# Sums over states three half steps late instead of two, a fifth state buffer, and softplus's product split into two stages

## The chip, the cores and the metric

The kernel runs on one core of a Trainium2 chip. Times are device microseconds of that core. Five things matter on it: the tensor engine (PE), which multiplies and transposes into the accumulation memory (PSUM, eight banks per partition); the vector engine (DVE); the scalar engine (ACT); GpSimd (POOL); and the queue of the sync engine (SP), which issues the transfers. Each engine works off its own instructions in the order in which the program holds them, and waits on semaphores of the others.

## The reference, cut to what matters

An image of 128 channels and 32 by 32 pixels goes through four layers, 32 images in all: a 3x3 convolution, a Mamba block that scans the 1024 pixels in four directions, an attention layer with two short Mamba blocks, and a small circuit. Layer 1 takes nearly all the time. For each direction it does this, with 256 inner channels `d` and 16 states `n`:

```python
uc = silu(conv(in_proj(x)))                      # 256 x 1024
dtr, Bt, Ct = split(x_proj @ uc)                 # 8, 16 and 16 rows
dt = softplus(dt_proj_w @ dtr + dt_proj_b)       # 256 x 1024
def step(h, t):                                  # over the 1024 pixels
    h = exp(dt[t] * A) * h + (dt[t] * uc[t]) * Bt[t]
    y[t] = sum over n of h[:, n] * Ct[t, n]
```

After that come `y + uc * D`, a gate with `silu(z)`, the output projection, and the sum over directions.

## The kernel before, in words

Channels lie on the 128 partitions and the 1024 pixels along the free axis, so the 256 inner channels make two halves `h`. A **half step** is one state `n` of one half of one direction: 16 x 2 = 32 half steps a direction, 128 an image, 4096 for layer 1, and 64 more for the attention layer. `Steps.run` walks through all of them in one long list. Half step `i` consists of

- `decay` (L633, ACT): `da = exp(dt * A)`, in one of five buffers;
- `spread` (L653 or L647, PE): the row `Bt[n]`, copied over the partitions into a pair of PSUM banks `bu`, of which there are two pairs. In 11 half steps of 32 (`TURNED`) ACT has already multiplied by `du` in transposed form (`scale`, L662), and PE only transposes;
- `input` (L669, DVE): `bu = du * bu`, in the 21 half steps that are not turned;
- `scan` (L677, DVE): the recurrence along 1024 pixels, from `da` and `bu` into a buffer `hh`;
- `weigh` (L686, POOL): `hh = hh * cc`, where `cc` is the row `Ct[n]`, loaded by SP (L625) into one of three buffers;
- `add` (L722, PE): eight transposes add `hh` to the sums `y` in two PSUM banks. For `n = 0`, `add` first starts `y` with the product of `uc` and `D` (L701), and the sum of that state follows an iteration later (`catch_up`). When `n = 15` is in, ACT copies `y` out (`evict`, L740).

The order within iteration `i` is written out: `evict`, `decay(i+3)`, the pending reads of PSUM, `spread(i+1)`, `catch_up`, `scan(i)`, pending reads, `input(i+1)`, then **a slot for other work**, `scale(i+4)`, `weigh(i)`, `add(i-2)`, `load(i+3)`. So in PE's queue the sum of state `i-2` stands right ahead of the spread of state `i+2`.

The slot is filled by `Plan.slot`. All work outside the scans is cut into `Stage`s, in streams with a start, an end and gaps: the projections of the next direction (L280, two stages of two products for each of four blocks), `small` (L299), `rates` (softplus: L377 and the lines to L411), `turns` (L434), the gates (L481), `finish` (L459), the convolution of the next image (L969, six stages of three products), the output projection (L1021). The planner goes by estimated costs per engine (`load_of` gives those of the half step itself) and by how near each stream's end is. It looks at no measured time: the result is a fixed order.

Stages that need PSUM take one of two `mm` banks with `k.mm()`. The reading of a bank by ACT or DVE is put off with `k.later` and emitted by `k.flush`, or at once when a third bank is asked for. In `rates` the first stage, `rate`, takes both banks in one slot: one product for each 512 pixels, each of which ACT then reads twice (L385 and L386).

Buffers are by tag: `BUFS` gives four to `hh`, two to `dbl` (the projected rows: `dtr`, `Bt`, `Ct`, which the two `rates` of a direction read), each of 4 KB a partition. In the attention layer a tile `t1` shares the tag `dbl`.

Of the kernel before, what the change touches and what calls it, by code (L numbers as in the profile page):

```python
# [23 lines left out]
DS = 16  # L24
# [142 lines left out]
class Work:  # L167


    BUFS = {  # L170
        "uc": 4, "dt": 3, "du": 3, "dut": 2, "parts": 2, "dbl": 2, "cc": 3, "da": 5, "hh": 4,
        "bt": 2, "but": 3,
    }

# [67 lines left out]
class Direction:  # L242
# [116 lines left out]
    def rates(self, h, at=0):  # L359

        k, m, T = self.k, self.m, self.T
        nc = k.nc
        t = {}

        def new(tag):
            return k.work.tile([P, T], F32, tag=tag, name=tag)

        def rate():  # L370
            self.dt[h], self.du[h] = new("dt"), new("du")
            t["relu"], t["w"] = new("relu"), new("w")
            k.rating = True
            for c, cs in enumerate(self.chunks):
                at = 32 * (2 * h + c)
                ps = k.mm(self.ch)
                nc.tensor.matmul(  # L377
                    ps, m.dw[at : at + 32, h * P : (h + 1) * P], self.dbl[at : at + 32, cs],
                    start=True, stop=True,
                )  # L380
                k.later(parted(cs, ps))

        def parted(cs, ps):
            def run():
                nc.scalar.activation(self.du[h][:, cs], ps, AF.Abs)  # L385
                nc.scalar.activation(t["relu"][:, cs], ps, AF.Relu)  # L386
            return run

        def expo():
            k.exps()  # L390
            nc.scalar.activation(self.du[h], self.du[h], AF.Exp, scale=-1.0)

        def rounded():
            nc.scalar.activation(t["w"], self.du[h], AF.Identity, bias=k.one)
            nc.scalar.activation(t["w"], t["w"], AF.Identity, bias=k.less)  # L395

        def log():
            k.exps()
            nc.scalar.activation(self.dt[h], self.du[h], AF.Ln, bias=k.one)

        def lost():
            nc.gpsimd.tensor_tensor(t["w"], t["w"], self.du[h], ALU.subtract)  # L402

        def whole(name, op, last=False):
            def run():
                nc.gpsimd.tensor_tensor(self.dt[h], self.dt[h], t[name], op)  # L406
                k.rating = not last
            return run

        def weighed():  # L410
            nc.gpsimd.tensor_tensor(self.du[h], self.dt[h], self.uc[h], ALU.mult)  # L411

        return [
            Stage(rate, pe=1.2, act=2.4, takes=True, at=at, when=lambda: not k.rating),
            Stage(expo, act=1.2, gap=2),
            Stage(rounded, act=2.3), Stage(log, act=1.2), Stage(lost, pool=2.4),
            Stage(whole("relu", ALU.add), pool=2.4), Stage(whole("w", ALU.subtract, True), pool=2.4),
            Stage(weighed, pool=2.4),
        ]
# [135 lines left out]
class Steps:  # L555
# [11 lines left out]
    def run(self, ways, plan):  # L567

        k = self.k
        steps = [(w, h, n) for w in ways for h in range(2) for n in range(DS)]  # L570
        self.steps = steps
        for i in range(3):
            self.load(i)
        for i in range(3):
            self.decay(i)
        self.spread(0)
        self.input(0)
        for i in range(len(steps) + 2):
# [12 lines left out]
            self.add(i - 2)  # L591
            self.load(i + 3)
        self.evict()
        k.flush()
# [4 lines left out]

    def load_of(self, i):  # L600

        n = (i - 2) % DS
        pe, act, pool, dve = 1.05, 1.15, 2.4, 2.3
        if n < 2:

            pe += 1.05
        if n == 0:
            act += 1.2
        if self.has(i + 1):
            pe += 1.0 if self.turned(i + 1) else 0.5  # L610
# [132 lines left out]
class Kernel:  # L743
# [173 lines left out]
    def images(self):  # L917
        tc, nc, d = self.tc, self.nc, self.d
        with ExitStack() as ctx:
# [162 lines left out]
            images, ways, plan = [], [], Plan(self)  # L1082
# [20 lines left out]
            with tc.manual_schedule():  # L1103
                w = ways[0]
# [10 lines left out]
                each = Steps.SLOTS  # L1115
                for k, w in enumerate(ways):
                    j, q = divmod(k, 4)
                    at = k * each
                    if w.last:
                        plan.add(w.gates(), at - 11, at + 14)  # L1120
                        plan.add(w.finish(0), at + 19, at + 31)
                    if q == 2:
                        plan.add(ways[k - 1].finish(1) + way_out(images[j], ways[k - 1]), at + 3, at + 16)
                    if q == 0 and j:
                        plan.add(ways[k - 1].finish(1) + way_out(images[j - 1], ways[k - 1]), at + 3, at + 16)
# [13 lines left out]
    def attention(self):  # L1139
# [4 lines left out]
        with ExitStack() as ctx:  # L1144
# [14 lines left out]
            chunks = [(c, slice(c * ch, (c + 1) * ch)) for c in range(T // ch)]  # L1159
            biases = [self.vec("L2_conv_convh_b"), self.vec("L2_conv_convw_b")]  # L1160
            g8s, ways = [], []
            both8 = self.work.tile([8, 2, T], F32, tag="carry", name="g8")
            for a, m in enumerate(ms):
# [6 lines left out]
                for c, cs in chunks:  # L1170
# [5 lines left out]
                        self, m, 0, taps, lambda c, taps=taps: taps(3, c), view, T, segment=S  # L1176
# [59 lines left out]
            with tc.manual_schedule():  # L1236
                each = Steps.SLOTS
# [7 lines left out]
                for a, w in enumerate(ways):  # L1245
                    plan.add(w.gates(), a * (each + 8) + 1, a * each + 14)
                    plan.add(maps(a), a * each + 4, a * each + 28)
                    plan.add(w.finish(0), a * each + 19, a * each + 31)
# [3 lines left out]
                plan.add(ways[0].finish(1) + way_out[: len(chunks)], each + 3, each + 9)  # L1252
                plan.add(way_out[len(chunks) :], each + 10, 2 * each - 2)
# [294 lines left out]
```

## Time and profile before

| | us |
|---|---|
| median of 3 runs | 15073.83 (15066.03 to 15084.82) |
| the profiled execution, its own time | 15093.06 |
| its span, first to last instruction | 15091.3 |
| busy: PE / DVE / ACT / POOL | 13174.8 / 13401.1 / 12256.2 / 12747.8 |
| mean granted clock of PE | 0.92 |

Busy times are over the whole span. The forty slices of the page are even from the second on (DVE 9 or 8 tenths, PE 8) until the last three, where the circuit runs. In groups of the page, "busy, mean ns" is the time of the group and of one instruction; what follows the bar is the idle time of the engine just ahead of these instructions and who ended it. A product of f32 appears as two rows of PE. Matmuls are pipelined, so the mean of one row is longer than the distance from row to row. The starts of one image's scans follow those of the last by 443.8 us in most images.

### The profile page before, as it was taken

The numbers are of one execution on the slowest core, as the hardware profiler recorded it, in microseconds if no ns is written. First come the engines' busy times: TensorE is split into PE (matmuls) and PEld (weight loads), VectorE is DVE, ScalarE is ACT, GpSimd is POOL, SyncE is SP. The second block draws the span as 40 slices with busy tenths as digits, with TensorE's granted clock in tenths as the row PEclk, the third lists the DMA queues.
The fourth block names the chain that finished last, engine by engine and source line by source line (L and its number), as shares of the span: only waits on it lengthen the run. The fifth ranks groups of instructions, "written<-read, shape, count | busy, mean of one in ns | idle before, by whom it ended". The sixth has DMA issues, their size and how long they took to land. (4 is left out here: it accounts for less than half of the span.)

```text
span 15091.3 us, 197699 instructions
## 1 busy us (share of the span) xinstructions
PE 13174.8 (87%) x70318; PEld 8507.7 (56%) x70318; DVE 13401.1 (89%) x8776; ACT 12256.2 (81%) x21181; POOL 12747.8 (84%) x6529
## 2 busy tenths in 40 slices
PE   7888888888888888988888888888888888888876
PEld 4555555555555555555555555555555555555532
DVE  7999989999989999898999999999999999999774
ACT  6888888888888888888888888888888888888642
POOL 6888888888888888888888888888888888888764
PEclk8999999999999999999999999999999999999877
DMA  3444444444444444444444444444444444444431
GB/s 118 159 155 155 156 153 154 156 159 156 155 153 153 158 155 159 154 154 154 153 157 159 154 157 153 155 152 158 157 157 154 155 153 154 157 159 157 144 107 68
DMA packets 633895, 2277.61 MB, mean 151 GB/s; under 512 B 77481, under 2 KB 81145, under 8 KB 632777
## 3 DMA queue, kind: packets, MB, share of 16 engines
q1 hardware_dynamic: 630600, 2263.06, 43.8%
q8 instruction: 554, 9.08, 0.2%
q14 instruction: 437, 3.57, 0.1%
q10 hardware_dynamic: 2304, 1.90, 0.0%
HBM read 2221.35 MB, written 43.33 MB: 150 GB/s over the span
## 5 line engine op out<-in xcount | busy, mean ns | idle before, releaser
L686 POOL TENSOR_TENSOR hh<-hh,cc 128x1024 f32<-128x1024 f32 x4160 | 9771.8, 2366 | 1752.5 <-DVE hh L677 1086.5
L677 DVE TENSOR_TENSOR_SCAN hh<-da,bu 128x1024 f32<-128x1024 f32 x4160 | 9415.4, 2280 | 618.6 <-PE bu L647 234.9
L722 PEld LDWEIGHTS y<-cbig,hh 128*128 128x128 f32 x33280 | 4065.2, 150 | 1793.5 <-issue 1285.2
L722 PE MATMUL y<-cbig,hh 128*128 128x128 f32 x33280 | 4762.6, 290 | 181.8 <-POOL hh L686 181.4
L633 ACT ACTIVATE da<-dt,m_na 128x1024 f32<-128x1024 f32 x4096 | 4607.2, 1144 | 352.8 <-DVE hh L677 344.9
L669 DVE TENSOR_TENSOR bu<-du,bu 128x1024 f32<-128x1024 f32 x2752 | 3336.8, 1213 | 680.5 <-PE bu L653 679.6
L662 ACT ACTIVATE but<-dut,bt 128x128 f32<-128x128 f32 x11264 | 3433.6, 392 | 0.0
L653 PE MATMUL bu<-parts,sel 48*128 48x512 bf16 x5504 | 1761.5, 402 | 638.6 <-DVE hh L677 630.0
L280 PE MATMUL mm<-hpad,m_wc 128*128 128x512 f32 x4096 | 2063.6, 627 | 104.1 <-ACT relu L386 68.6
L647 PE MATMUL bu<-cbig,but 128*128 128x128 f32 x11264 | 1606.7, 290 | 378.1 <-DVE hh L677 331.6
L647 PEld LDWEIGHTS bu<-cbig,but 128*128 128x128 f32 x11264 | 1388.4, 151 | 445.2 <-issue 287.8
L280 PEld LDWEIGHTS mm<-hpad,m_wc 128*128 128x128 f32 x4096 | 710.1, 193 | 908.6 <-issue 753.5
L653 PEld LDWEIGHTS <-sel 48*128 48x128 bf16 x5504 | 322.6, 95 | 1149.9 <-DVE hh L677 687.2
L402 POOL TENSOR_TENSOR w<-w,du 128x1024 f32<-128x1024 f32 x260 | 613.8, 2361 | 38.3 <-ACT w L395 38.3
L299 PE MATMUL mm<-uc,m_xw 128*128 128x512 f32 x1024 | 602.9, 720 | 31.0 <-ACT sz L762 22.6
L701 PEld LDWEIGHTS y<-m_skip,uc 128*128 128x128 f32 x4096 | 554.4, 212 | 132.8 <-issue 79.8
L762 ACT ACT_TABLE_LOAD x483 | 619.7, 1283 | 8.5
L768 ACT ACT_TABLE_LOAD x483 | 619.7, 1283 | 8.5
L439 ACT COPY dut<-mm 128x512 f32<-128x512 f32 x512 | 294.9, 576 | 407.0 <-PE mm L434 406.9
L406 POOL TENSOR_TENSOR dt<-dt,w 128x1024 f32<-128x1024 f32 x260 | 615.3, 2366 | 0.2
L411 POOL TENSOR_TENSOR du<-dt,uc 128x1024 f32<-128x1024 f32 x260 | 614.3, 2363 | 0.2
L406 POOL TENSOR_TENSOR dt<-dt,relu 128x1024 f32<-128x1024 f32 x260 | 613.9, 2361 | 0.0
(219 smaller groups left out, 10394.3 us busy)
## 6 DMA issues: line engine op xcount, KB each, us to landing
cc<-rows SPq DMA_DIRECT2D x4160, 512.0 KB, 3.8
xt<-in_x SPq DMA_DIRECT2D x32, 512.0 KB, 5.9
x<-xt SPq DMA_DIRECT2D x32, 512.0 KB, 3.7
xt<-x SPq DMA_DIRECT2D x32, 512.0 KB, 4.0
out<-xt SPq DMA_DIRECT2D x32, 512.0 KB, 2.9
rows<-dbl SPq DMA_DIRECT2D x130, 64.0 KB, 4.3
stats<-st SPq DMA_DIRECT2D x32, 36.0 KB, 1.5
means<-stats SPq DMA_DIRECT2D x1, 1152.0 KB
```

The costliest lines, as they stand in the source:

```text
L280: nc.tensor.matmul(self.view(ps), m.wc[:, v, j, h * P : (h + 1) * P], self.taps(j, c), start=(j == 0), stop=(j == 3),)
L406: nc.gpsimd.tensor_tensor(self.dt[h], self.dt[h], t[name], op)
L633: k.nc.scalar.activation(t, w.dt[h], AF.Exp, scale=w.m.na[:, h, n : n + 1])
L647: k.nc.tensor.matmul(t[:, b * P : (b + 1) * P], but[:, b], k.ident, start=True, stop=True, is_transpose=True,)
L653: k.nc.tensor.matmul(t[:, cs], k.sel[:, n], w.parts[:, cs], start=True, stop=True)
L662: k.nc.scalar.activation(t[:, b], w.dut[h][:, b], AF.Copy, scale=w.bt[:, b, n : n + 1])
L669: k.nc.vector.tensor_tensor(t, w.du[h], t, ALU.mult)
L677: k.nc.vector.tensor_tensor_scan(way(t), way(self.da.pop(i)), way(self.bu.pop(i)), 0.0, ALU.mult, ALU.add)
L686: k.nc.gpsimd.tensor_tensor(t, t, self.cc.pop(i), ALU.mult)
L722: k.nc.tensor.matmul(self.y[g][: w.bl, b], t[:, at], k.ident, start=False, stop=(n == DS - 1 and b == w.per - 1), is_transpose=True,)
L762: self.nc.scalar.activation(*args, AF.Silu, **kw)
L768: self.nc.scalar.preload_act_table_set("natural_log_exp_and_others")
```

## The change

Three things are changed.

1. `add(i - 2)` becomes `add(i - 3)`; the loop of `run` goes one iteration further, and `load_of` takes its `n` from `i - 3`. `hh` gets a fifth buffer, so that a state may be kept one half step longer. `dbl` gives its second buffer for it.
2. `rate` is now two stages, one for each 512 pixels, with one bank each; the planner is told 0.9 of PE and 1.2 of ACT for each (it was 1.2 and 2.4 for both).
3. The streams that read finished sums (`finish`, `way_out`, `end`) start one slot later, and most of their ends move by one.

```diff
-        "uc": 4, "dt": 3, "du": 3, "dut": 2, "parts": 2, "dbl": 2, "cc": 3, "da": 5, "hh": 4,
+        "uc": 4, "dt": 3, "du": 3, "dut": 2, "parts": 2, "dbl": 1, "cc": 3, "da": 5, "hh": 5,
...
-        def rate():
-            self.dt[h], self.du[h] = new("dt"), new("du")
-            t["relu"], t["w"] = new("relu"), new("w")
-            k.rating = True
-            for c, cs in enumerate(self.chunks):
+        def rate(c, cs):
+            def run():
+                if c == 0:
+                    self.dt[h], self.du[h] = new("dt"), new("du")
+                    t["relu"], t["w"] = new("relu"), new("w")
+                    k.rating = True
                 at = 32 * (2 * h + c)
                 ps = k.mm(self.ch)
...
-            Stage(rate, pe=1.2, act=2.4, takes=True, at=at, when=lambda: not k.rating),
+            *(
+                Stage(rate(c, cs), pe=0.9, act=1.2, takes=True, at=at, when=lambda c=c: c or not k.rating)
+                for c, cs in enumerate(self.chunks)
+            ),
...
-        for i in range(len(steps) + 2):
+        for i in range(len(steps) + 3):
...
-            self.add(i - 2)
+            self.add(i - 3)
...
-        n = (i - 2) % DS
+        n = (i - 3) % DS
...
-                        plan.add(w.finish(0), at + 19, at + 31)
+                        plan.add(w.finish(0), at + 20, at + 31)
...
-                        plan.add(ways[k - 1].finish(1) + way_out(images[j], ways[k - 1]), at + 3, at + 16)
+                        plan.add(ways[k - 1].finish(1) + way_out(images[j], ways[k - 1]), at + 4, at + 17)
...
-                        plan.add(end(images[j - 1]), at + 17, at + 44)
+                        plan.add(end(images[j - 1]), at + 18, at + 45)
```

The remaining lines of the diff make the same shift by one for the other `way_out` of layer 1 and for `finish` and `way_out` of the attention layer.

More of the change, by code (lines that the diff above doesn't have):

```diff
@@ L381, in rate @@
                 k.later(parted(cs, ps))
+            return run
         def parted(cs, ps):
@@ L1120, in images @@
                         plan.add(w.gates(), at - 11, at + 14)
-                        plan.add(w.finish(0), at + 19, at + 31)
+                        plan.add(w.finish(0), at + 20, at + 31)
                     if q == 2:
-                        plan.add(ways[k - 1].finish(1) + way_out(images[j], ways[k - 1]), at + 3, at + 16)
+                        plan.add(ways[k - 1].finish(1) + way_out(images[j], ways[k - 1]), at + 4, at + 17)
                     if q == 0 and j:
-                        plan.add(ways[k - 1].finish(1) + way_out(images[j - 1], ways[k - 1]), at + 3, at + 16)
-                        plan.add(end(images[j - 1]), at + 17, at + 44)
+                        plan.add(ways[k - 1].finish(1) + way_out(images[j - 1], ways[k - 1]), at + 4, at + 17)
+                        plan.add(end(images[j - 1]), at + 18, at + 45)
                     if q == 1 and j + 1 < self.n:
@@ L1247, in attention @@
                     plan.add(maps(a), a * each + 4, a * each + 28)
-                    plan.add(w.finish(0), a * each + 19, a * each + 31)
+                    plan.add(w.finish(0), a * each + 20, a * each + 31)
                 plan.add(ahead[begun:], 1, each - 2)
@@ L1251, in attention @@
                 way_out = out(0)
-                plan.add(ways[0].finish(1) + way_out[: len(chunks)], each + 3, each + 9)
-                plan.add(way_out[len(chunks) :], each + 10, 2 * each - 2)
+                plan.add(ways[0].finish(1) + way_out[: len(chunks)], each + 4, each + 10)
+                plan.add(way_out[len(chunks) :], each + 11, 2 * each - 2)
                 Steps(self).run(ways, plan)
```

## The prediction

> **What bounds the kernel now.** I read the page's busy times first, then its groups, then the waits of DVE and of PE, then one image in windows, then the timeline of its worst places. From the page:
>
> ```profile
> PE 13174.8 (87%) x70318; PEld 8507.7 (56%) x70318; DVE 13401.1 (89%) x8776; ACT 12256.2 (81%) x21181; POOL 12747.8 (84%) x6529
> ...
> L686 POOL TENSOR_TENSOR hh<-hh,cc 128x1024 f32<-128x1024 f32 x4160 | 9771.8, 2366 | 1752.5 <-DVE hh L677 1086.5
> L677 DVE TENSOR_TENSOR_SCAN hh<-da,bu 128x1024 f32<-128x1024 f32 x4160 | 9415.4, 2280 | 618.6 <-PE bu L647 234.9
> L669 DVE TENSOR_TENSOR bu<-du,bu 128x1024 f32<-128x1024 f32 x2752 | 3336.8, 1213 | 680.5 <-PE bu L653 679.6
> ```
>
> All engines are 81 to 89% busy; none is full. DVE sets the pace: POOL mostly waits for its scans (1086.5 us), and DVE waits for PE's spreads. The waits:
>
> ```profile
> DVE bu L669 <- PE bu L653: 679.6, 520, 53.9
> DVE hh L677 <- PE bu L647: 234.9, 185, 2.7
> ...
> PE y L722 <- POOL hh L686: 181.4, 168, 3.0
> PE mm L280 <- ACT relu L386: 68.6, 31, 2.2
> PE mm L459 <- ACT uc L762: 68.1, 31, 2.3
> ```
>
> The first two (total, times, longest, us) are what the change can win: 914.5 us, less 53.9 for the start, is 860.6 us or 27 us an image. The next three are times when PE itself stood. Only the third is on POOL; the fourth, 31 times 2.2 us, comes once an image. So PE's own load must make most of DVE's wait. One image and five stretches of it (columns: length, then busy PE, PEld, DVE, ACT, POOL):
>
> ```profile
> 4536.00:4980.00 444.00, 391.18 (x2164) 255.18 (x2162) 407.12 (x251) 377.34 (x656) 389.33 (x198) 0.95 0.47 157
> 4603.00:4616.00 13.00, 13.00 (x73) 8.24 (x72) 10.15 (x7) 8.23 (x18) 13.00 (x7) 1.00 0.35 110
> 4659.00:4669.00 10.00, 10.00 (x60) 7.27 (x61) 7.42 (x6) 5.96 (x13) 9.76 (x7) 0.96 0.34 109
> 4741.00:4779.00 38.00, 35.50 (x152) 20.33 (x151) 26.50 (x17) 28.87 (x50) 24.18 (x12) 0.96 0.39 132
> 4827.00:4845.00 18.00, 15.70 (x106) 11.08 (x104) 14.53 (x10) 16.82 (x31) 10.66 (x5) 1.00 0.46 149
> 4868.00:4881.00 13.00, 11.91 (x66) 7.44 (x65) 11.49 (x7) 11.20 (x12) 12.73 (x6) 1.00 0.57 192
> ```
>
> DVE idles 36.9 us in the image, and 2.85, 2.58, 11.50, 3.47 and 1.51 us of it in these five stretches (A to E). In A, B and C PE is full: too much other work fell into a few half steps. D and E show PE standing:
>
> ```profile
> 4830.79 1.13 PE L377 MATMUL mm<-dbl,m_dw 32*128 32x512 f32 x4
> ...
> 4835.03 0.61 ACT L386 ACTIVATE relu<-mm 128x512 f32<-128x512 f32 x1
> ...
> 4835.69 1.98 PE L280 MATMUL mm<-hpad,m_wc 128*128 128x512 f32 x4 [2.21 <-ACT relu L386]
> ...
> 4840.03 1.23 DVE L669 TENSOR_TENSOR bu<-du,bu 128x1024 f32<-128x1024 f32 x1 [1.66 <-PE bu L653]
> ...
> 4869.36 1.10 PE L722 MATMUL y<-cbig,hh 128*128 128x128 f32 x8 [1.09 <-POOL hh L686]
> ...
> 4871.03 1.23 DVE L669 TENSOR_TENSOR bu<-du,bu 128x1024 f32<-128x1024 f32 x1 [0.34 <-PE bu L653]
> ```
>
> In D softplus has both banks, the next projection waits 2.21 us for one, and DVE's product is late. In E the sum waits 1.09 us for POOL, but only 0.34 us of that reaches DVE.
>
> **What the Trainium skill says.** "Perfetto Trace Analysis", section Identifying Performance Opportunities, has the busiest of the vector, scalar and GpSimd engines as the one to follow through its gaps, and takes repeated gaps as a sign that buffers may be short: DVE at 89% with gaps that recur in each image agrees. The same page, section Matmuls, wants independent products to rotate through PSUM banks so that one is read while the next is filled: stretch D shows what it costs where they don't. "TensorE: Matmul & The Clock Gate", Part 1, has PE at half clock after an idle window of some 3.4 us; here the mean granted clock is 0.92, and in this image eight transposes of a sum take 1.91 us after PE's wait of 2.29 us on ACT in stretch C, 1.03 elsewhere. A wait of PE is thus paid twice in places.
>
> **The change part by part.** No work is removed: both built programs hold the same PE, DVE and POOL instructions. ACT gets two more switches each way between its tables, 4 x 1.283 us (rows L762 and L768), hidden in an engine 81% busy. I count per image, times 31 (32 less start and end).
>
> *Sums three behind.* Each sum asks for POOL's result one half step later. An unhindered half step lasts 3.5 us with a product (1.21 + 2.28) and about 2.2 without, against a longest wait of 3.0 us, so nearly all of PE's 181.4 us of waiting goes. What is it worth? Bounds: all 181, if each microsecond reached DVE, and 57, what I get by following DVE's late instructions back through PE's queue to such waits. I take 60. Behind the waiting sum stands the spread of state `i+2`, for which DVE waits; later are then only POOL's own tasks, which have slots of margin. The scan's wait for a free `hh` doesn't change: it needs the sum of `i-5` (was `i-4`), issued in iteration `i-2` both times. SP's loads wait on `weigh`, which isn't moved.
>
> *One buffer for `dbl`.* Its next writer is ACT after `small`, at half steps 1, 34, 68 and 99 of the new order; the last reader, the second product of `rates(1)`, stands at 127, 26, 58 and 92, two or more earlier in PE's own queue, and the transfer of the rows (4.3 us) some 25 half steps before. Cost nothing; if that cover were gone, PE's order alone would still put reader ahead of writer. `t1` comes 16 half steps after the last reader.
>
> *Two stages of softplus.* The work is the same, but no stage holds both banks. The wait of 2.2 us (68.6 in all) goes: the first product stands at 80, the second at 81, the next projection at 87. But in half step 80 the planner now puts an image product, the second output projection and the first softplus product together, some 0.9 + 1.9 + 0.9 us, and the output projection still waits for DVE (59.1 us in all, 1.9 an image). D goes from a mean of 4.9 over the images to about 3: 1.9 x 31 = 58.
>
> *The new order, C.* In half steps 58 to 66 PE has about 14.5 us of spreads and sums (9 x 1.5, plus turned ones). Before, it also has six convolution stages (2.74 each), two projection stages (1.9 each), a `finish` and two `turns` (1.8 together), softplus (1.85) and a start of `y` (1.95): 25.8, plus 2.3 of waiting. DVE needs 28.5. 42.6 less 28.5, less some 3 that PE may be ahead, is 11: the 11.5 seen. In the new order these half steps hold 20.4: 34.9 less 28.5 less 3 is 3.4. But stages five and six, the start of `y` and both `small` (1.88 each) then fall into 67 to 70, some 11 us against 2 before. I take 8 for all of C: 3.5 x 31 = 108.
>
> *The new order, A and B.* The four projection stages of A move from 18, 19, 20, 21 to 18, 19, 21, 22, and the next four from 24 to 27 to 28 to 31: PE has no run left that exceeds DVE's pace by 3. A goes from 3.0 to 0.5: 78. In B `small` and the gate no longer share a half step: 2.5 to 1, 47. On the other side, at 124 to 0 of the next image and at 93 to 96, projection, `turn` and the second softplus product now meet, 2.7 to 3.3 above DVE's pace: I add 2.3, -71.
>
> Sum: 60 + 58 + 108 + 78 + 47 - 71 = 280 us. Waits taken from one place partly come back in the next, and I see the ones that vanish better than the ones that appear; I keep three quarters, 210. From the span, 15091.3 - 210 = 14881; the profiled execution (15093.06) stood 19 above the median, so **14865 us**, 1.4% less.
>
> **Rivals.**
>
> *Only the cured waits count (20%).* The planner's order is as crowded as before, since the same PE work must fit between the same scans, and only POOL's and softplus's waits go, a part of 181 + 69: 60 to 90 us, about 15000. For it: C's work moves by a few half steps and doesn't go. Against: A and B thin out.
>
> *More than that (12%).* PE keeps its clock, and most of the 27 us an image goes: DVE's own work and bubbles need 416, so half of the rest, 13 x 31 = 400 us, gives 14670.
>
> *No difference (8%).* DVE's waits move one for one into the new crowds: 15074.
>
> *Slower (12%).* The crowd at 66 to 70 meets a PE at half clock. It now follows light half steps (56 to 58 hold 0.4 to 0.9 us of other work each), in which PE stands. About 22 us of PE work stand there; at half clock throughout, they cost up to 22 more. It decides the sign from 7 us an image on, that is if PE stays at half clock for some 14 us of those 22; at 10 us it gives 15170. For it: the clock was 0.63 from 4749 to 4753 us, in C, right after a wait. Against: over the whole of each of the five stretches it is 0.96 or 1.00 (the column after POOL).
>
> **How the numbers follow.** My forecast (14750 to 14980) has 48%. Runs here spread by 19 us, 0.13%, so 0.2% or 30 us is about what a measurement can tell from no change. Faster by that: 48 + 20 + 12 = 80%; within: 8%; slower: 12%. For 8 in 10 I leave out half of the strongest gain below and most of the slower case above: 14710 to 15075.
>
> **What would show it.** Right: PE's wait on `hh` L686 near nothing; that of L280 on L386 gone; DVE's two waits on spreads down from 914 to about 700; POOL's and DVE's busy times unchanged; an image in about 437 us; the largest gap late in C, at half steps 66 to 70. Wrong: DVE's waits on L653 as large as before with PE full around them (first rival), or PE's rows at twice the distance there (slower).

## The result: no difference

| | before | after |
|---|---|---|
| median of 12 runs, us | 15078.97 (15066.03 to 15084.82) | 15085.10 (15047.41 to 15099.89) |
| the profiled execution, its own time | 15093.06 | 15085.33 |
| its span | 15091.3 | 15083.2 |
| mean granted clock of PE | 0.92 | 0.918 |

The ratio of the times is 1.0000, with a 95% interval from 0.9991 to 1.0009. The forecast was 14865 us, a gain of 1.4%. The likeliest case (14750 to 14980) and the wider range (14710 to 15075) both miss, and the case that came true ("no difference") had a chance of 8%.

In the changed kernel the lines after softplus stand five further down: L686 is L691, L677 is L682, L722 is L727, L1021 is L1026. The page after, busy times and costliest groups:

```profile
PE 13325.4 (88%) x70318; PEld 8474.9 (56%) x70318; DVE 13424.2 (89%) x8776; ACT 12262.2 (81%) x21185; POOL 12759.8 (85%) x6529
...
L691 POOL TENSOR_TENSOR hh<-hh,cc 128x1024 f32<-128x1024 f32 x4160 | 9781.5, 2368 | 1800.8 <-DVE hh L682 1037.6
L682 DVE TENSOR_TENSOR_SCAN hh<-da,bu 128x1024 f32<-128x1024 f32 x4160 | 9416.1, 2281 | 767.4 <-PE bu L652 224.5
L674 DVE TENSOR_TENSOR bu<-du,bu 128x1024 f32<-128x1024 f32 x2752 | 3335.6, 1212 | 426.3 <-PE bu L658 422.3
```

DVE's idle time ahead of its products fell from 680.5 to 426.3 us, as it should. Ahead of its scans it rose, from 618.6 to 767.4, though the spreads' part of that did not. So something else is late. The waits of DVE (total, times, longest, us):

```profile
DVE bu L674 <- PE bu L658: 422.3, 350, 53.3
DVE hh L682 <- PE bu L652: 224.5, 125, 7.0
...
DVE hh L682 <- PE y L727: 122.6, 95, 2.8
...
DVE o L1032 <- PE mm L1026: 94.6, 33, 3.9
```

The two waits on spreads fell from 914.5 to 646.8 us, by 268, even further than the 700 that the prediction named as its sign. The third row was not among the waits before; the fourth was 3.6 us there. These two take back 214. Four smaller ones (the scan on an image product of L852, on the scaled rows of L667 and on softplus's `du`, and L986 on L974) rose by some 48 more, DVE's busy time rose by 23, and its wait on the gates' product (L465) lost 23. That closes the balance within a few us of the span's 8: DVE idles 39.3 us an image before and 39.0 after, as a mean over the images. And the waits of PE:

```profile
PE mm L974 <- ACT xpad L961: 95.1, 31, 4.3
PE mm L997 <- ACT parts L345: 79.1, 31, 2.8
...
PE mm L280 <- ACT relu L388: 31.1, 31, 1.0
...
PE y L727 <- POOL hh L691: 8.8, 5, 3.0
```

The wait on POOL that the late sums were to cure is gone (181.4 to 8.8). That of the projection on softplus, 2.2 us at half step 83 of each image, is gone from its place; the 31.1 us are another wait, of 1.0 us, at half step 94. The first two rows are new: once an image PE stands 3.1 us for the padded input of the convolution (`xpad`; 2.7 us in the whole run before), and once 2.5 us for a bank that ACT reads. One image in windows (length; busy PE, PEld, DVE, ACT, POOL; clock; DMA share; GB/s), and of it stretch C (half steps 57 to 71) and D (79 to 82):

```profile
4521.00:4964.00 443.00, 397.51 (x2142) 256.51 (x2141) 402.22 (x248) 373.27 (x652) 385.12 (x196) 0.93 0.47 155
...
4713.00:4774.00 61.00, 56.99 (x276) 34.10 (x274) 45.82 (x29) 44.61 (x76) 47.75 (x24) 0.94 0.41 138
4799.00:4819.00 20.00, 16.94 (x64) 8.81 (x61) 13.77 (x10) 13.31 (x26) 9.72 (x7) 0.83 0.31 106
```

The kernel before, the same half steps 57 to 71, and 79 to 85:

```profile
4737.00:4798.00 61.00, 55.80 (x272) 34.22 (x271) 48.95 (x31) 42.75 (x74) 46.62 (x22) 0.96 0.40 130
4819.00:4846.00 27.00, 22.11 (x131) 14.42 (x131) 23.39 (x15) 23.88 (x45) 18.48 (x8) 1.00 0.43 145
```

In C DVE idles 15.2 us of 61 where it idled 12.1. In D it idles 6.2 us of 20, at a clock of 0.83; before, 3.6 of the longer 27 at 1.00. As means over the images, half steps 57 to 71 hold 13.0 us of DVE's idle time before and 14.7 after, and half steps 79 to 85 hold 5.4 and 6.4. The largest gap of a single half step is in D, at 81, and the timeline shows it (start, duration, engine; in brackets the idle time ahead and who ended it):

```profile
4805.18 1.18 PE L997 MATMUL mm<-g,nin 128*128 128x512 f32 x2 [2.52 <-ACT parts L345]
...
4806.15 1.91 PE L727 MATMUL y<-cbig,hh 128*128 128x128 f32 x8
...
4809.06 1.23 DVE L674 TENSOR_TENSOR bu<-du,bu 128x1024 f32<-128x1024 f32 x1 [2.43 <-PE bu L658]
...
4810.82 2.94 PE L1026 MATMUL mm<-sz,m_ow 128*128 128x512 f32 x4
...
4813.80 0.69 DVE L1032 SCALAR_TENSOR_TENSOR o<-mm,hpad 128x512 f32<-128x512 f32 x1 [3.51 <-PE mm L1026]
...
4814.41 2.28 DVE L682 TENSOR_TENSOR_SCAN hh<-da,bu 128x1024 f32<-128x1024 f32 x1
```

In half step 80 the planner put the next image's product (L997), the second output projection (L1026) and the first softplus product (L378). All three take `mm` banks. PE stands 2.52 us for a bank that ACT has still to read (for the other L997, of half step 79), and then runs slowly: the eight transposes of a sum take 1.91 us (1.10 eight us later), the two products of the output projection 2.94 (1.88 ten us earlier). The third request for a bank makes the program emit the pending read of the output projection at once, and this read (L1032) is DVE's. So it stands in DVE's queue ahead of scan 81, and the scan, whose own spread is in, waits 3.51 us for an output projection that nobody needs so soon.

The next largest gap is in C, at half step 61:

```profile
4723.44 4.90 PE L974 MATMUL mm<-xpad,w 128*128 128x512 f32 x6 [4.01 <-ACT xpad L961]
...
4730.22 2.29 DVE L682 TENSOR_TENSOR_SCAN hh<-da,bu 128x1024 f32<-128x1024 f32 x1 [5.28 <-PE bu L652]
...
4730.36 2.74 PE L974 MATMUL mm<-xpad,w 128*128 128x512 f32 x6
```

```profile
4719.40:4730.00 10.60, 6.59 (x24) 3.81 (x24) 5.41 (x3) 7.86 (x15) 9.57 (x6) 0.68 0.44 151
```

The new order puts the first stage of the convolution at half step 59, where it stood at 60, and its input isn't ready. PE stands 4.01 us and then needs 4.90 us for the stage's three products, while those of the next stage take 2.74, at a clock of 0.68 over these 10.6 us. The spread behind them is late, and scan 61 waits 5.28 us. The images of this one trace can be compared: in 5 of 30 (the first and last left out) the stage waits only 1.1 us and takes 2.84, DVE idles 0.6 us at half step 61, and the image lasts 436.9 us. In the other 25 it waits 1.6 to 4.3 us and takes 4.4 to 5.0, DVE idles 4.8 us there, and the image lasts 444.2 us as a mean. Half step 61 is 4.2 of these 7.2 us. What makes an image one or the other isn't shown. The gap is a wait that the trace names and a clock that falls with it, so the two theories below don't exclude each other.

### The profile page after: what moved, and what is told of

Read it like the earlier page. It is cut to its first block, busy times and chain, and to the rows that moved or that the text cites. A ratio compares the mean times of both kernels' runs of the same rounds, so it can differ in the third digit from the quotient of the medians.

```text
span 15083.2 us, 197375 instructions
## 1 busy us (share of the span) xinstructions
PE 13325.4 (88%) x70318; PEld 8474.9 (56%) x70318; DVE 13424.2 (89%) x8776; ACT 12262.2 (81%) x21185; POOL 12759.8 (85%) x6529
## 4 chain that ended last, share of the span: by engine, by line
PE 33%; ACT 26%; DVE 23%; issue 10%; POOL 7%; DMA 1%; DVEq 0%; SPq 0%; POOLq 0%; ACTq 0%
DVE hh L682 15%; ACT da L638 8%; PE y L727 7%; ACT but L667 7%; PE mm L280 6%; DVE bu L674 6%; POOL hh L691 5%; PE mm L974 4%; PE bu L652 3%; PE bu L658 3%; ACT L773 2%; PE mm L378 2%; PE mm L299 2%; PE y L706 1%; ACT L767 1%
## 5 line engine op out<-in xcount | busy, mean ns | idle before, releaser
L691 POOL TENSOR_TENSOR hh<-hh,cc 128x1024 f32<-128x1024 f32 x4160 | 9781.5, 2368 | 1800.8 <-DVE hh L682 1037.6
L682 DVE TENSOR_TENSOR_SCAN hh<-da,bu 128x1024 f32<-128x1024 f32 x4160 | 9416.1, 2281 | 767.4 <-PE bu L652 224.5
L727 PEld LDWEIGHTS y<-cbig,hh 128*128 128x128 f32 x33280 | 4048.6, 149 | 1578.8 <-issue 1263.2
L727 PE MATMUL y<-cbig,hh 128*128 128x128 f32 x33280 | 4683.4, 288 | 8.8 <-POOL hh L691 8.8
L674 DVE TENSOR_TENSOR bu<-du,bu 128x1024 f32<-128x1024 f32 x2752 | 3335.6, 1212 | 426.3 <-PE bu L658 422.3
L667 ACT ACTIVATE but<-dut,bt 128x128 f32<-128x128 f32 x11264 | 3434.8, 392 | 0.0
L280 PE MATMUL mm<-hpad,m_wc 128*128 128x512 f32 x4096 | 2047.1, 623 | 44.5 <-ACT relu L388 31.1
L652 PEld LDWEIGHTS bu<-cbig,but 128*128 128x128 f32 x11264 | 1345.4, 149 | 574.6 <-ACT but L667 284.6
L974 PE MATMUL mm<-xpad,w 128*128 128x512 f32 x1152 | 586.3, 649 | 95.1 <-ACT xpad L961 95.1
L378 PE MATMUL mm<-dbl,m_dw 32*128 32x512 f32 x1024 | 640.3, 709 | 25.4 <-DVE sz L470 25.3
L706 PEld LDWEIGHTS y<-m_skip,uc 128*128 128x128 f32 x4096 | 490.4, 193 | 151.0 <-ACT back L745 50.2
```

The lines of the kernel that those rows point to most:

```text
L280: nc.tensor.matmul(self.view(ps), m.wc[:, v, j, h * P : (h + 1) * P], self.taps(j, c), start=(j == 0), stop=(j == 3),)
L378: nc.tensor.matmul(ps, m.dw[at : at + 32, h * P : (h + 1) * P], self.dbl[at : at + 32, cs], start=True, stop=True,)
L652: k.nc.tensor.matmul(t[:, b * P : (b + 1) * P], but[:, b], k.ident, start=True, stop=True, is_transpose=True,)
L667: k.nc.scalar.activation(t[:, b], w.dut[h][:, b], AF.Copy, scale=w.bt[:, b, n : n + 1])
L674: k.nc.vector.tensor_tensor(t, w.du[h], t, ALU.mult)
L682: k.nc.vector.tensor_tensor_scan(way(t), way(self.da.pop(i)), way(self.bu.pop(i)), 0.0, ALU.mult, ALU.add)
```

## The experiments

Two theories stood before the experiments. *Balance*: the late sums are worth something, and the split and the new order of the stages take it back, each by waits that the traces name. *Clock*: what is won turns into idle time of PE, PE falls to half clock more often, and the image stays as long whatever is cured.

### Each half of the change alone, and PE kept busy

`late_only` has the late sums and the shifted streams, with the old one-stage softplus. `split_only` is the kernel before with the split alone. In both, the planner decides anew. `warm_after` and `warm_before` put transposes of zeros onto the open sums `y` where PE waits (263 and 226 an image; the sums stay what they are), so that PE stands less.

```diff
+        if w.turned and i >= 128:
+            for _ in range(self.FILL.get(i % 128, 0)):
+                k.nc.tensor.matmul(
+                    self.y[0][:, 0], k.zero, k.ident, start=False, stop=False, is_transpose=True
+                )
         self.bu[i] = t = k.psb.tile([P, w.T], F32, tag="bu", name="bu")
```

> The change without the split of softplus: sums three behind, five state buffers, shifted streams, but one stage of softplus that takes both banks. Theory 1 (an image's time snaps to whole windows of the tensor engine's clock gate, 3.413 us, since the half-speed stretches move with the phase): images of 436.9, 440.3 or 443.8 us, total within 0.5% of before, PE's wait for POOL near nothing all the same. Theory 2 (the two parts cancel: late sums win, the split's crowded half step 80 loses): 15000 us or less, and no crowd at half step 80. Theory 3 (late sums win nothing and the split wins): about 15080.

> The kernel before with only softplus's product split into two stages. Theory 1: within 0.5% of before, most images again a whole number of 3.413 us windows. Theory 2 (the split is what loses): 15150 us or more, with the loss in the half step where the second output projection and the first softplus product meet. Theory 3: 15020 or less, since the wait of a projection for a bank that softplus holds (68.6 us in all before) goes.

> The changed kernel with transposes of a zero tile, added to the open sums y (which stay as they are), placed ahead of those spreads for which the tensor engine stands waiting for DVE or ACT: 263 an image, about 30 us at full clock, no more at any place than the mean wait there. Theory 1 (the half clock that follows these waits costs the time, and the clock gate's windows set an image's length): granted clock 0.96 or more, DVE's waits for spreads fall by half, an image takes 420 to 432 us and is no longer a whole number of windows, total 14550 to 14850. Theory 2 (only the crowded half steps matter, whatever the clock): 15050 to 15250, since PE gets more to do and nothing becomes shorter.

> The same filling of PE's waits in the kernel before: 226 zero transposes an image at its own waits. Theory 1: granted clock 0.96 or more, total 14550 to 14900, and the difference to the filled changed kernel shows what the change is worth when the clock is out of play: the changed one faster by 50 to 200 us. Theory 2: 15050 to 15250, and no difference between the two filled kernels.

| kernel | us (before: 15089.32) | ratio, 95% interval |
|---|---|---|
| late_only | 15229.59 | 1.0093 [1.0078, 1.0108] |
| split_only | 15140.18 | 1.0031 [1.0018, 1.0045] |
| warm_after | 14918.93 | 0.9887 [0.9871, 0.9904] |
| warm_before | 15011.71 | 0.9950 [0.9935, 0.9965] |

None of the three theories for `late_only` foresaw a loss of 140 us, and both filled kernels lie between the times of their two theories. Each half alone makes the kernel slower, and both together do not: the planner orders each of them anew, so these times hold the order as well as the edit. In `split_only` PE's wait for POOL at the sums grew from 181.4 to 385.9 us: the new order makes the wait that late sums cure. So these two runs can't price the halves, and the next ones keep the order fixed.

The filling works on both kernels, and the changed kernel is 93 us faster than the one before once both are filled, though not equally: their clocks are 0.960 and 0.948. PE is fuller by 344 us, and the kernel is faster by 166:

```profile
PE 13669.1 (92%) x78471; PEld 9059.9 (61%) x78471; DVE 13433.0 (90%) x8777; ACT 12280.0 (82%) x21185; POOL 12763.7 (86%) x6529
```

The clock views of `after` and of `warm_after`:

```profile
core 0: 15083.2 us, clock 0.918
```

```profile
core 0: 14919.1 us, clock 0.960
```

### The late sums in the old order, and three mendings

`same_order_late` is the kernel before with `add(i - 3)`, five `hh` and one `dbl`; `load_of` and the streams stay, so every stage keeps its half step. `swap` mends the third row of DVE's waits above: the sum of `n = 0` starts `y`, and the product of `uc` and `D` comes an iteration later. `out20` gives the output projections until three slots later, which takes them from half steps 79 and 80 to 81 and 83, and moves one product of `finish` by a half step. `warm_after_minus` is `warm_after` without the column sums of an image (their result is left zero), 1.99 us of DVE's work an image.

```diff
 # swap, in add and catch_up
-            for g, b, at in blocks:
-                nc.tensor.matmul(
-                    self.y[g][: w.bl, b], w.uc[h][:, at], m.skip[:, h], start=(b == 0), stop=False
-                )
+            self.sum(i)
             self.owed = i
...
-            self.sum(self.owed)
+            w, h, n = self.steps[self.owed]
+            for g, b, at in self.blocks(w):
+                self.k.nc.tensor.matmul(
+                    self.y[g][: w.bl, b], w.uc[h][:, at], w.m.skip[:, h], start=False, stop=False
+                )
...
 # out20, twice
-plan.add(ways[k - 1].finish(1) + way_out(images[j], ways[k - 1]), at + 4, at + 17)
+plan.add(ways[k - 1].finish(1) + way_out(images[j], ways[k - 1]), at + 4, at + 20)
```

> The kernel before with sums three behind, five state buffers and one for the projected rows, but with every stage in the same half step as before: the planner's costs and the streams' starts and ends are left as they were, and softplus stays one stage. Theory 1 (late sums are worth what the prediction said, and the loss of the run without the split, 140 us, came from the planner's new order): PE's wait for POOL goes and nothing else moves, 15000 to 15060 us. Theory 2 (late sums bring a wait of their own: the sum of a direction's first state, which catch_up issues behind the next spread, is now needed by a scan in half step 5 or 21 of a direction, where no product comes first; in the changed kernel DVE waits 122.6 us for it in all): DVE shows such a wait of 50 to 130 us, and the total is 15070 to 15150.

> The changed kernel in which the first state's sum starts y, and the product of uc and D is what catch_up adds an iteration later: the same instructions, the two exchanged, so that the first state's buffer comes free an iteration earlier. Theory 2: DVE's wait for the sum (122.6 us) vanishes, and the total falls by 60 to 120 us, to 14960 to 15020. Theory 1 with the clock gate's windows setting an image's length: the wait vanishes as well, but the total falls by 0 or by whole windows of 3.4 us in a part of the images, so anything from 14870 to 15085. Rival (the wait is covered by PE's lateness anyway): PE's spread becomes the last to come, DVE's waits in all stay as they are, 15070 to 15100.

> The changed kernel with the end of the streams of finish and output projection three slots later (20 in place of 17). This moves only the output projection and one finish product: half step 80 loses the output projection, which goes to 81 and 83. If that crowd costs what it seems to in the changed kernel (DVE stands 5.6 us before scan 81 in each image, and in the kernel before 1.6), the total falls by 60 to 130 us, to 14950 to 15025. If the clock gate's windows set the length, the stall before scan 81 shrinks all the same, and the total falls by whole windows in some images or not at all.

> The filled changed kernel without the sums over the image's columns (one reduction of 1.99 us of DVE an image; its result is left zero, so the attention layer gets other data). Filled, most images last 436.9 us, 128 windows of 3.413 us. If DVE's work sets the time, 1.99 x 32 = 64 us less than the filled kernel, 14855. If the windows hold the image's length, it stays within 25 us of the filled kernel's 14919, or drops by a whole window in most images, 3.4 x 31 = 106 us, to about 14815.

| kernel | us (before: 15082.86) | ratio, 95% interval |
|---|---|---|
| same_order_late | 14969.12 | 0.9929 [0.9914, 0.9943] |
| swap | 15051.56 | 0.9977 [0.9970, 0.9985] |
| out20 | 14999.55 | 0.9946 [0.9931, 0.9961] |
| warm_after_minus | 14909.68 | 0.9889 [0.9872, 0.9905] |

The late sums, alone and in the old order, are worth 114 us, more than either theory gave them. `late_only`, with the same late sums in the planner's new order, stood at 15230: the order and the later starts cost it some 250 us. The waits of `same_order_late`, of PE and then of DVE:

```profile
PE y L722 <- POOL hh L686: 28.5, 38, 3.0
```

```profile
DVE bu L669 <- PE bu L653: 588.1, 382, 53.7
...
DVE hh L677 <- PE y L722: 96.6, 62, 3.0
...
DVE hh L677 <- PE bu L647: 45.1, 40, 2.7
```

The gain shows in the waits on spreads, 914.5 to 633.2 us; the second row is the price of late sums, here too. Its cause is in the code: for `n = 0` the sum of state `s` is issued by `catch_up`, behind the spread of the very half step whose scan reuses the buffer. Before, that was half step 4 or 20 of a direction, where DVE still has a product ahead of the scan, and the product hid the sum. With five buffers it is half step 5 or 21, both in `TURNED`, with no product. In `swap` the wait on `y` is gone from DVE's list. The two that are left stand higher than after (422.3 and 224.5), so only part of the 122.6 is won, 34 us, where 60 to 120 was expected. At half step 69 the gap shrinks from 2.75 to 0.97 us, and at 70 it grows from 2.70 to 4.49:

```profile
DVE bu L674 <- PE bu L658: 467.1, 399, 54.1
DVE hh L682 <- PE bu L652: 232.8, 153, 8.6
```

`out20` gives 86 us, within the 60 to 130 expected, and its wait of L1032 is 2.2 us where it was 94.6:

```profile
DVE o L1032 <- PE mm L1026: 2.2, 2, 1.2
```

Half steps 79 to 85 now hold 3.4 us of DVE's idle time an image, where they held 6.4. Not all of the gain lies there: at half step 61, where no stage was moved, the gap fell from 4.3 to 2.1 us, and at others it rose.

`warm_after_minus` is the odd one. 1.99 us less of the pacing engine's work an image, 62 us in all, moved the median by 9, and the ratio to the kernel before not at all (0.9887 and 0.9889). What it says of the clock is taken up at the end.

### The split in the old order

In `same_split` and `same_late_split` softplus's second product is held back and issued at the start of the next slot; every stage keeps its half step. The first stands on the kernel before, the second on `same_order_late`. `same_late_swap` is `same_order_late` with the swap, `warm_same_late_swap` that with filling (310 an image).

```diff
-            for c, cs in enumerate(self.chunks):
-                at = 32 * (2 * h + c)
-                ps = k.mm(self.ch)
...
-                k.later(parted(cs, ps))
+            product(0, self.chunks[0])
+            k.todo.extend(lambda c=c, cs=cs: product(c, cs) for c, cs in enumerate(self.chunks) if c)
+
+        def product(c, cs):
+            at = 32 * (2 * h + c)
+            ps = k.mm(self.ch)
...
+            k.later(parted(cs, ps))
```

> The kernel before with softplus's product split as in the change, but every stage in the half step of before: the planner sees one stage at the old cost, and the second product is issued at the start of the next slot. Sums stay two behind. Theory 1 (the split itself is worth the bank wait that it removes, and the loss of 51 us in the run with the split alone came from the new order): PE's wait of L280 for L386 (68.6 us) goes, 15000 to 15050 us. Theory 2 (the split itself loses, as the second product now stands in a half step with other work): 15100 or more.

> All of the change but its order: sums three behind, five state buffers, one for the projected rows, softplus's product split, and every stage in the half step of before. Late sums alone in this order gave 14969. Theory 1 (both parts are worth something by themselves, and the planner's new order alone cost the change its gain): 14890 to 14960, some 130 to 190 us below the changed kernel. Theory 2 (the parts get in each other's way): 14980 or more.

> Late sums in the order of before (14969), with the first state's sum and the product of uc and D exchanged. There DVE waits 96.6 us for that sum. Theory 1 (a wait of its own that late sums bring): the wait goes and the total falls by 50 to 100 us, to 14870 to 14920. Theory 2 (PE's next spread is late anyway, or the clock gate's windows hold the length): it goes, and the total falls by less than 40 us, to 14930 to 14969.

> The same, with zero transposes in the waits that PE has in the run with late sums in the order of before (310 an image, 35 us at full clock). Theory 1 (half clock costs what filling can win back, 70 to 170 us as in the two filled kernels): granted clock 0.96 or more, 14770 to 14870. Theory 2 (with these waits removed PE's lateness no longer counts): no less than 30 us below the kernel without filling.

| kernel | us (before: 15081.66) | ratio, 95% interval |
|---|---|---|
| same_split | 15155.28 | 1.0044 [1.0027, 1.0061] |
| same_late_split | 15007.92 | 0.9952 [0.9937, 0.9967] |
| same_late_swap | 14938.47 | 0.9905 [0.9891, 0.9920] |
| warm_same_late_swap | 14890.02 | 0.9873 [0.9859, 0.9888] |

The split, with its second product in the next half step and nothing else moved, costs 74 us on the kernel before. On top of the late sums it is 39, of two medians from different batches, and their intervals (±22 us each) leave its size open, not much its sign. A later place for the second product wasn't tried in the old order. DVE's waits on spreads in `same_split` are 991 us, 76 more than the 914.5 before:

```profile
DVE bu L677 <- PE bu L661: 677.0, 443, 53.5
DVE hh L685 <- PE bu L655: 314.0, 227, 2.6
```

In `same_split` the projection at half step 83 still waits for softplus, 36.1 us in all in place of 68.6, and gaps of DVE grew at half steps 62, 63, 73, 93 and 125. With late sums and no split this wait is down to 4.5 us; with the split, in `same_late_split`, it is 45.5 us again, now at half step 94, and at 95 DVE idles 3.4 us an image where it idled none. One stage that held two banks for one half step has become a stage in each of two half steps, and the traces show the second one meeting other takers of a bank.

The swap gives 31 us in this order too, as its second theory said. Filling on top of it gives 48 us, and 14890 misses the 14870 of its first theory.

### The best of them, and one more test of the clock

`warm_swap_out20` is the changed kernel with swap, `out20` and filling. `warm_same_swap_out` is `same_order_late` with the swap, filling, and the output projections' end moved from slot 16 to 20. `after_plus` is the changed kernel with an image's row sums made twice, 1.19 us more of DVE's work an image.

```diff
 # warm_same_swap_out, twice
-plan.add(ways[k - 1].finish(1) + way_out(images[j], ways[k - 1]), at + 3, at + 16)
+plan.add(ways[k - 1].finish(1) + way_out(images[j], ways[k - 1]), at + 3, at + 20)
 # after_plus
-Stage(rows, dve=1.3, gap=2)
+Stage(lambda: (rows(), rows()), dve=1.3, gap=2)
```

> The changed kernel with one reduction of an image's rows done twice (1.19 us more of DVE an image, the same result). If DVE's work sets the time, 38 us more: 15123. If the length of an image snaps to whole windows of the clock gate (most images of the changed kernel last 130 of them), it stays within 15 us of the changed kernel, or moves by whole windows: 3.4 us in a part of the images.

> The changed kernel with three mendings at once: the first state's sum exchanged with the product of uc and D (31 us alone), the later end of the output projection's stream (83 us alone), and the filling of PE's waits (166 us alone), with the filling placed as in the filled changed kernel. If they add up: 14800. If each works on the same lateness of PE: no better than the best alone by more than 40 us, 14880 to 14919.

> Late sums in the order of before, exchanged first sum, filled waits (together 14890), and the later end of the output projection's stream, which moves it from half steps 78 and 79 to 79 and 80, and softplus from 81 to 80. If the crowd there costs as in the changed kernel: 14800 to 14860. If the order of before has no such crowd to mend, or the windows hold the image's length: 14875 to 14910.

| kernel | us (before: 15069.93) | ratio, 95% interval |
|---|---|---|
| after_plus | 15096.18 | 1.0019 [1.0012, 1.0025] |
| warm_swap_out20 | 14873.93 | 0.9871 [0.9856, 0.9885] |
| warm_same_swap_out | 14847.75 | 0.9850 [0.9833, 0.9866] |

`warm_same_swap_out` is faster than both kernels by about 1.5%. It has the late sums and the fifth buffer of the change, and neither the split nor the new order. In `warm_swap_out20` the three mendings of the changed kernel give 211 us together by the medians (some 195 by the ratio to before), where alone they gave 34, 86 and 166: these three don't add up. The filling was not placed anew for the waits that the other two leave.

## Why the prediction was wrong, step by step

The table walks from the kernel before to the changed one by medians, against 15082 us, about the median of before in these batches. The three parts add up to the whole by the way they are made, so their sum proves nothing, and their sizes depend on the order of the walk: with the split first it is +74, and the late sums after it -147.

| step | forecast, us | measured, us | from |
|---|---|---|---|
| sums three behind | -60 (bounds -57, -181) | -114 | same_order_late |
| two stages of softplus | -58 | +39 | same_late_split against same_order_late |
| the new order (A, B, C, and the meetings at 93 to 96 and 124 to 0) | -162 | +77 | after against same_late_split |
| sum | -280, of which 210 kept | +2 | |

The other account is by place. It gives DVE's idle time an image as a mean over the images, us:

| place (half steps) | before | after | difference | forecast |
|---|---|---|---|---|
| A (18 to 31) | 4.4 | 1.5 | -2.9 | -2.5 |
| B (36, 37) | 2.6 | 0.9 | -1.7 | -1.5 |
| C (57 to 71) | 13.0 | 14.7 | +1.7 | -3.5 |
| D (79 to 85) | 5.4 | 6.4 | +1.0 | -1.9 |
| meetings (93 to 96, 124 to 0) | 1.9 | 3.4 | +1.5 | +2.3 |
| half step 114 | 0.0 | 1.6 | +1.6 | none |
| whole image | 39.3 | 39.0 | -0.3 | |

**The steps that failed are C and D.** They were to win 5.4 us an image and lost 2.7; over 31 images that is about 250 us, nearly the 280 of the sum.

*Sums three behind: right, undersized.* The wait went as foretold. The value of 60 came from following single late instructions of DVE back to it; 114 lies in the middle of the bounds. One sentence in this step was false, "the scan's wait for a free `hh` doesn't change". It holds for 15 states of 16. For `n = 0` the sum is issued an iteration later, and the turned half steps 5 and 21 have nothing to cover it: 122.6 us of waiting, and the swap won back 34 us here and 31 in the old order. The prediction counted in which iteration a sum is issued, and not behind which spread.

*One buffer for `dbl`: right.* No wait for it is in the trace. ACT's two more table switches each way didn't show either.

*Two stages of softplus, D: the sign was wrong.* The step said "the wait of 2.2 us goes" since the next projection stood seven half steps off, and that wait did go. But it took the split to be free elsewhere: the second stage meets another projection at half step 94, and the split alone costs 74 us. Nor was the split needed for D: the late sums alone, in the old order, bring half steps 79 to 85 from 5.4 to 3.3 us. And for D the step said "from 4.9 to about 3". The means over the images are 5.1 before (1.60 and 3.51 us, at half steps 81 and 84) and 5.6 after, all at half step 81: about 3.1 of it for the output projection's read and 2.5 for a late spread. The step had named the crowd in half step 80 and added up PE's load in it. It didn't ask in which queue the forced read of a bank would stand. `out20`, which moves the output projections out of this crowd, gives 86 us.

*The new order, C: wrong.* The step took C from 11.5 to 8 us in the image shown; the means are 13.0 and 14.7. For half steps 58 to 66 it reckoned 34.9 us of PE's work (14.5 and 20.4), which left 3.4 of idle time. In the sum for the old order stand 2.3 us of PE's waiting; in that for the new order it put the waiting at nothing, without a reason, and took all work at full clock. The trace has 8.5 us of idle time there. Ahead of scan 61 PE waits 3.1 us an image for the convolution's input, and the stage then takes 4.6 us as a mean, where it takes 2.8 at full clock. These two, 4.9 us together, are about the 5.1 that the sum lacks; this match is an estimate, and no run with the convolution placed later was made. The late part was named ("the largest gap late in C") and is 6.0 us at half steps 67 to 70, where 4.6 was taken. Its two gaps stand at half steps 69 and 70 (2.75 and 2.70 us). For C the prediction summed PE's work over several half steps, as if PE could even it out within them; the gaps come from single half steps. The changed kernel's timeline at half step 69:

```profile
4759.31 1.95 PE L706 MATMUL y<-m_skip,uc 128*128 128x128 f32 x16
...
4761.96 1.04 PE L727 MATMUL y<-cbig,hh 128*128 128x128 f32 x8
4763.13 2.29 DVE L682 TENSOR_TENSOR_SCAN hh<-da,bu 128x1024 f32<-128x1024 f32 x1 [2.75 <-PE y L727]
```

The start of `y`, a spread and the sum of `n = 0` stand in a row, and the scan waits for the last of them: the false sentence above meets the late crowd.

*A and B: right.* The table has both within 0.4 us of the forecast. The meetings cost 1.5 us where 2.3 was taken, but half step 114, which the prediction doesn't name, lost another 1.6, and 46 won 1.2.

*The rival "slower by half clock"* asked whether PE would fall to half clock in the crowd at 66 to 70. It did not: after 4730 us the clock in C is 1.00. But the rival came near: it had light half steps in which PE stands, and then PE's work at half clock. It came at half steps 59 to 61, right behind the light ones that the rival names, and in D. The mean over C, 0.94, hides it. Over the whole run 2424 us of before's span and 2461 of after's passed at half clock, so that the change as a whole hardly added to it; in `same_order_late`, where the gain is, it is 49.6 us an image against 60.7.

The sign by which the forecast was to be judged, DVE's two waits on spreads at about 700 us, came true (647), and the time didn't move. The sign was too narrow: it watched the waits that should shrink and not the sum of DVE's idle time.

## What to carry to other kernels

Where a planner places the work, price an edit in the old order first (here -114 and +39 us) and the new order on its own (+77), since the order can be worth as much as the edit. Ask of each stage that the new order moves forward whether its input is there, and read the clock in short windows: 0.94 over 61 us hid 0.68 over 10.6. When a buffer is kept longer, look for the one state whose release is issued differently, and at what covers it in the half step that it moves to. When stages compete for banks, ask of each forced read in whose queue it will stand: here one stood ahead of a scan on the pacing engine and held it back 3.51 us.

## What the runs showed that had not been expected

**Added work on PE made the kernel faster.** PE's busy time is 344 us longer with the zero transposes, and the kernel 166 us shorter (1.1%), with the clock up from 0.918 to 0.960. On the kernel before it is 78 us, with 0.920 to 0.948. That the clock is the way is the plain reading; zero transposes where PE doesn't wait weren't tried as a comparison. The gap at half step 61 stays (4.9 us), since PE waits and slows down there in the filled kernel too.

**The length of an image tends to whole steps of the clock.** The clock in the records takes only the values 1.0 and 0.5, and its half-speed stretches come in units of 3.413 us. From the end of one image's last scan to the next, the commonest length is about 443.75 us both before and after (11 of 27 images each): 130.0 of these units. In `warm_after`, where no whole numbers were expected, 17 of 27 images are within 0.06 of a whole number, all of them at 128; in `warm_same_late_swap` 19. By chance it would be some 3 of 27. In the changed kernel the 5 images in which the convolution at half step 59 runs at full clock are those of 128.0 units. In `swap`, `out20` and `warm_after_minus` long and short images mostly alternate, and a pair often comes to 259.0, 258.0 and 256.0. This fits what was odd above: `warm_after_minus`, with 1.99 us less of DVE's work an image, has a mean image of 437.0 us against 437.2. A cure smaller than a unit might be lost to this, or return as more. It isn't settled how far it explains the result. `late_only` has no image on a whole number, `same_order_late` 8 of 27, and their times moved by 140 and 114 us. `after_plus` was to decide it and did so only in part: its commonest image stayed at 443.73 us (18 of 27 on whole numbers), with 1.19 us more of DVE's work in each; but its time is 0.19% above the kernel before, 29 us with an interval of 18 to 38, and the whole of the added work (1.19 x 31 = 37 us) lies within that; its median is only 11 us above that of the changed kernel in an earlier batch. What ties the image to the units, and whether the balance of the table above would close in the same way without that, stays open.
